# A four-layer convolution block: buffers, and the place of side work in its interleaved stages

## The chip, the cores and the metric

The kernel runs on one core of a Trainium2 chip. The metric is the device time of one launch in microseconds (us). Three runs of the kernel before took 5979.35, 5992.16 and 6012.22 us; their median is 5992.16 us.

## The reference

The input x is 16 images of 64 x 64 tokens with 256 channels, all fp32. Four layers follow one another. Each takes the group norm of x (32 groups of 8 channels, over the whole image) and adds its result to x.

```python
def _gn(v, G=32, eps=1e-5):
    ...
# layer 0: the nearest of 1024 code vectors replaces each token
dis = sum(xf*xf) + sum(e*e) - 2 * xf @ e;  out0 = e.T[argmin(dis)]
# layer 1: attention within each image row of 64 tokens, sigmoid instead of softmax
out1 = sigmoid(f @ g.T) @ h          # f, g: 32 channels, h: 256
# layer 2: a rank-one attention over all 4096 tokens of an image
sm = softmax(x0[:, :, None] * x1[:, None, :], axis=1)
out2 = sigmoid(einsum('bn,bnm->bm', x2, sm)) * x
# layer 3: linear attention with 4 heads of 32 channels, then a layer norm
q = softmax(q over channels) * 32**-0.5;  k = softmax(k over tokens)
out3 = layernorm((k v^T)^T q @ w_out + b_out) * gamma + beta
x = x + out_i(_gn(x))                # for i = 0, 1, 2, 3
```

## The kernel before, in words

**Tiling.** An image (a "batch", b = 0 to 15) has 4096 tokens. It is cut into 8 chunks of 512 tokens (`NCHUNK`, `CW`), and a chunk into 4 token tiles of 128 (`CH`, `P`). Between the layers x lies in DRAM in transposed form, one tile of 128 partitions x 2 channel halves x 512 tokens per chunk (512 KB): x1 after layer 0, x2 after layer 1, x3 after layer 2.

**Stages.** Each stage of a batch is a Python generator. It emits instructions and yields a number of units. `stats0` takes the statistics of the input. `stage1` is the search of layer 0: per token tile four matmuls against the codes (line 382), a sum with the negated norms and a maximum on VectorE (line 389), the index of the maximum (line 394), and a gather of the code vector that is added onto the token tile by an indirect DMA of GpSimd (line 395). Its side work per chunk is `norm` (the normalized tile and its squares, lines 327 and 330, and the row norms), `norm_rows` (a small copy, line 348, which the bias of line 377 reads), `back` (transposes of the finished tokens, line 357, their copy, line 360, the statistics and the store of x1) and the two loads `load` and `tokens` (lines 317 and 321). `layer1` computes per chunk f and g (line 465), h (lines 476 to 485), the scores and their sigmoid (lines 494 to 500) in `attend`, then the attention product and the sum in `mix` (lines 509 and 513). `rows2` projects x2 onto three vectors, each chunk into its own 32 columns of PE (line 567). `stage2` goes over 32 token tiles x 2 halves of the image: ScalarE makes 2048 exponentials per partition with their sum (line 619), VectorE multiplies them by the third projection and sums (line 622); both write the same tile `ex`. `gate2` applies the gate (lines 675 and 676) and stores x3. `stage3` is layer 3: a first pass over the chunks computes k, q and v, the exponentials of k with a running maximum, the softmax of q per head, and the sum of k v products; a second pass (`form`, `variance` and the loop after them) makes the output from the stored q tiles, the small matrix `wctx` and x3.

**The q softmax** (lines 768 to 776) takes a maximum on VectorE (770), a subtraction on GpSimd (771), an exponential on ScalarE (772), a sum and a reciprocal on VectorE (774, 775) and a product on GpSimd (776). In the kernel before all of it is emitted in one piece after the transposes of k (line 762) and `queries(ch - 1)`, which transposes the q tile of the chunk before (line 717) and stores it to DRAM through ScalarE's queue.

**What orders the work.** At the end of the kernel a list of tasks gives each stage of each batch a start and a length, in units of one batch. A heap always resumes the task with the smallest time; a resumed task moves on by length x yielded units / total. So the stages of up to five batches are emitted interleaved. `LEN1`, `LENG` and `LEN3` are lengths of layer 1, the gate and layer 3; `total` of layer 1 is 88 in the kernel before. A compile-time scheduler then puts the instructions of each engine in a fixed order: in the order of emission where an instruction is ready by its own estimate, and a later one first where it is not. `tc.high_priority` puts a few ahead (the ends of the group-norm statistics, `gn_finish`, lines 261 to 277). [...] All loads and most stores are issued from SyncE's queue (SP), which waits at an issue whose buffer is not free yet.

**Buffers.** A tile with a `tag` shares `bufs` slots with the others of this tag; a new tile waits for the last reader of its slot. `t4` (5 slots of 4 KB a partition) holds the negated norms `nn` and the distances `nd` of the search, the squares `sq`, layer 1's `fg` and the projections `rows`. `v2` (5 slots of 2 KB) holds layer 3's `kx`, `ek`, `qT` and `qz`. `ex` has 2 slots of 8 KB, `h` 2 of 4 KB, `xb` 3 of 4 KB (loads of the statistics, the rows and layer 3), `qo` 2. The PSUM tiles of 1024 columns (`wide`: `pd` of the search, `ph` and `po` of layer 1) share 2 slots.

Of the kernel before, what the change touches and what calls it, by code (L numbers as in the profile page):

```python
# [35 lines left out]
LAG3, LENG = 0.06, 0.8  # L36
LAG4 = 0.04
LEN3 = {0: 0.4, 1: 0.33, 2: 0.37}
# [3 lines left out]
def kernel(  # L42
# [55 lines left out]
    neg_mat = s1p.tile([P, P], F32, tag="t4", name="neg_mat", bufs=5)  # L98
# [92 lines left out]
    gam = s3p.tile([P, C], F32, tag="v2", name="gam", bufs=5)  # L191
# [116 lines left out]
    def stage1(b):  # L308
# [14 lines left out]
        def norm(ch):  # L323
            xn[ch] = s1p.tile([P, NK, CW], F32, tag="xn", name=f"xn_{tag}_{ch}")
            sq = s1p.tile([P, NK, CW], F32, tag="t4", name=f"sq_{tag}_{ch}", bufs=5)
# [46 lines left out]
        for ch in range(NCHUNK):  # L372
            for t in range(CH):
                T = ch * CH + t

                nn = s1p.tile([P, CODES], F32, tag="t4", name=f"nn_{tag}_{T}", bufs=5)
# [10 lines left out]
                nd = s1p.tile([P, CODES], F32, tag="t4", name=f"nd_{tag}_{T}", bufs=5)  # L387
# [13 lines left out]
                if t == 1:  # L401
                    if ch + 1 < NCHUNK:
                        norm(ch + 1)
                        yield 2
                if t == 2:
                    if ch + 1 < NCHUNK:
                        norm_rows(ch + 1)
                    if ch > 0:
                        back(ch - 1)
                        yield 2  # L410
                if t == 3:
                    if ch + 1 < NCHUNK:
                        tokens(ch + 1)
# [10 lines left out]
    def layer1(b):  # L424
# [34 lines left out]
        def attend(ch):  # L459
# [9 lines left out]
            fg = s1p.tile([2 * CK, 2, HW], F32, tag="t4", name=f"fg_{tag}_{ch}", bufs=5)  # L469
# [3 lines left out]
            ph = wide(f"ph_{tag}_{ch}").rearrange("p (t c) -> p t c", c=C)  # L473
            for t in range(CH):
                for k in range(NK):
                    nc.tensor.matmul(  # L476
                        ph[:, t, :], lhsT=X[:, k, t * P : (t + 1) * P], rhs=wh_n[:, k, :],
                        start=(t % 2 == 0 and k == 0), stop=False, skip_group_check=True,
                    )
                if t % 2 == 1:  # L480
                    nc.tensor.matmul(
                        ph[:, t - 1 : t + 1, :], lhsT=ones3, rhs=h_row, start=False, stop=True, skip_group_check=True
                    )
            hs[ch] = s1p.tile([P, CH, C], F32, tag="h", name=f"h_{tag}_{ch}")
            nc.scalar.copy(hs[ch], ph)
            yield 5
# [203 lines left out]
    def stage3(b):  # L690
# [33 lines left out]
        for ch in range(NCHUNK):  # L724
# [40 lines left out]
            if ch > 0:  # L765
                queries(ch - 1)
# [173 lines left out]
```

## Time and profile before

| | |
|---|---|
| median of three runs | 5992.16 us |
| time of the profiled execution | 5985.76 us |
| its span | 5984.0 us |
| mean granted clock of TensorE | 0.949 |
| busy PE / DVE / ACT / POOL | 5310.6 / 5132.9 / 4756.8 / 1873.7 us |
| instructions on PE / DVE / ACT / POOL | 25167 / 7270 / 7138 / 1314 |
| last search matmul (line 382) | 5209 us |

PE is TensorE's matmuls, PEld its weight loads, DVE VectorE, ACT ScalarE, POOL GpSimd, SP SyncE. The busy time of an engine leaves out its waits. The page lists an engine's idle time by the instruction that stood at the head of its queue and by what ended the wait. An fp32 matmul appears as two records (4096 for the 2048 of the search), a transpose as one. The costliest groups are these (mean ns of one instruction, and how many):

| group | ns | count |
|---|---|---|
| L622 DVE product and sum of the exponentials | 2318 (and 82 for reading the sum) | 1024 |
| L619 ACT exponentials | 2089 (and 190 for reading the sum) | 1024 |
| L382 PE search matmul, records | 621 each, 2013.5 us together | 4096 |
| L389, L394 DVE maximum and its index | 1212, 1218 | 512 each |
| L377 ACT negated norms | 1145 | 512 |

The profile of the steady part repeats from batch to batch: search matmuls of successive batches begin at 3455, 3808, 4162 and 4514 us.

### The profile page before, as it was taken

How to read it: one execution, taken by the hardware profiler on the slowest of the kernel's cores; microseconds unless marked ns; L12 is line 12 of the kernel's file. 1: busy time of each engine (PE TensorE's matmuls, PEld its weight loads, DVE VectorE, ACT ScalarE, POOL GpSimd, SP SyncE). 2: the span in 40 equal slices, each digit the busy share in tenths (PEclk: the TensorE clock that was granted, in tenths of full speed). 3: DMA queues.
4: the chain of work that ended last, by engine and by line, in shares of the span. 5: the costliest groups of instructions: out<-in, count | busy, mean ns of one | idle time of the engine just before them, and what ended most of it. 6: DMA issues, size and time to landing. Idle time of an engine off the chain costs nothing.

```text
span 5984.0 us, 73947 instructions
## 1 busy us (share of the span) xinstructions
PE 5310.6 (89%) x25167; PEld 3208.0 (54%) x25167; DVE 5132.9 (86%) x7270; ACT 4756.8 (79%) x7138; POOL 1873.7 (31%) x1314
## 2 busy tenths in 40 slices
PE   8978798989989899998989989898999989887777
PEld 3535355545556465554646556464655646464445
DVE  6589698899989899898989989898998989888862
ACT  4578597878888797888979788797988879787763
POOL 3222224233332333323333332433333333312231
PEclk9989899999999999999999999999999999998788
DMA  6453645665656657565665746566475655545543
GB/s 185 143 160 112 209 132 186 187 187 158 207 165 201 194 160 227 149 210 163 197 212 156 224 151 207 172 199 203 153 223 160 204 183 172 188 140 176 170 144 111
DMA packets 521359, 1059.10 MB, mean 177 GB/s; under 512 B 52504, under 2 KB 266392, under 8 KB 512792
## 3 DMA queue, kind: packets, MB, share of 16 engines
q1 hardware_dynamic: 406288, 885.11, 44.6%
q0 software_dynamic: 73728, 67.14, 7.8%
q10 hardware_dynamic: 40968, 102.13, 4.5%
q8 instruction: 200, 3.28, 0.2%
q14 instruction: 175, 1.43, 0.1%
HBM read 751.18 MB, written 303.04 MB: 176 GB/s over the span
## 4 chain that ended last, share of the span: by engine, by line
PE 48%; DVE 21%; ACT 15%; issue 7%; DMA 5%; POOL 4%; ACTq 0%; SPq 0%; POOLq 0%; DVEq 0%
PE pd_s L382 16%; DVE ex_s L622 10%; ACT ex_s L619 6%; PE ph_l L476 4%; PE pqv_s L751 4%; PE po_s L849 3%; DVE i_s L394 2%; PE pk_s L729 2%; PE pr_r L567 2%; DVE nd_s L389 2%; PE po_l L509 2%; POOL xc_s L395 2%; PE pvr_s L829 1%; DVE st_s L254 1%; PE pc_s L780 1%
## 5 line engine op out<-in xcount | busy, mean ns | idle before, releaser
L622 DVE CUSTOM_DVE_ANT_0 ex_s<-ex_s,x2b 128x2048 f32<-128x2048 f32 x1024 | 2369.4, 2318 | 135.9 <-ACT ex_s L619 133.5
L619 ACT ACTIVATE ex_s<-x0b,nmax_s,x_r 128x2048 f32<-128x2048 f32 x1024 | 2138.8, 2089 | 64.7 <-DVE num_s L622 55.0
L382 PE MATMUL pd_s<-e,xn_s 128*128 128x512 f32 x4096 | 2013.5, 621 | 87.6 <-DVE m L389 63.8
L395 POOL DMA_INDIRECT xc_s<-in_emb_rows,i_s x512 | 1084.0, 2117 | 1962.9 <-DVE i_s L394 1460.6
L382 PEld LDWEIGHTS pd_s<-e,xn_s 128*128 128x128 f32 x4096 | 750.6, 196 | 830.4 <-issue 655.0
L389 DVE CUSTOM_DVE_ANT_0 nd_s<-pd_s,nn_s 128x1024 f32<-128x1024 f32 x512 | 620.5, 1212 | 114.8 <-PE pd_s L382 85.4
L394 DVE FIND_INDEX8 i_s<-m,nd_s 128x8 uint32<-128x1024 f32 x512 | 623.5, 1218 | 0.0
L377 ACT ACTIVATE nn_s<-ne,nx_s 128x1024 f32<-128x1024 f32 x512 | 585.1, 1145 | 10.6 <-DVE nx_s L348 3.4
L476 PE MATMUL ph_l<-wh_l,xt_l 128*128 128x256 f32 x2048 | 534.6, 396 | 28.6 <-DVE xt_l L513 20.6
L751 PE MATMUL pqv_s<-wqv_s,xk_s 128*128 128x256 f32 x2048 | 491.9, 381 | 2.9 <-ACT xt_s L360 2.9
L476 PEld LDWEIGHTS ph_l<-wh_l,xt_l 128*128 128x128 f32 x2048 | 381.7, 194 | 155.1 <-issue 61.2
L751 PEld LDWEIGHTS pqv_s<-wqv_s,xk_s 128*128 128x128 f32 x2048 | 388.4, 191 | 130.1 <-issue 63.3
L832 POOL TENSOR_TENSOR lrs_s<-lrs_s,mhalf 128x4 f32<-128x4 f32 x128 | 187.6, 1465 | 651.5 <-ACT lrs_s L831 638.0
L849 PE MATMUL po_s<-wctx_s,qo_s 128*128 128x256 f32 x1024 | 329.4, 412 | 63.5 <-ACT y_s L852 59.8
L852 ACT ACTIVATE y_s<-po_s,lrs_s 128x256 f32<-128x256 f32 x512 | 236.0, 470 | 147.5 <-PE po_s L849 104.3
L327 ACT ACTIVATE xn_s<-xt_s,nb_n,s_n 128x512 f32<-128x512 f32 x256 | 202.4, 806 | 108.2 <-DMA xt_s<-in_xT 98.6
L776 POOL TENSOR_TENSOR qv_s<-qv_s,qd_s 128x512 f32<-128x512 f32 x128 | 167.2, 1307 | 385.3 <-DVE qd_s L775 312.8
L509 PE MATMUL po_l<-attn,h_l 128*128 128x128 f32 x2048 | 280.7, 283 | 7.3 <-DVE m L389 5.2
L509 PEld LDWEIGHTS po_l<-attn,h_l 128*128 128x128 f32 x2048 | 259.9, 195 | 45.8 <-issue 22.1
L849 PEld LDWEIGHTS po_s<-wctx_s,qo_s 128*128 128x128 f32 x1024 | 178.0, 199 | 194.5 <-ACT y_s L852 123.9
L729 PE MATMUL pk_s<-xk_s,wk_s 128*128 128x512 f32 x512 | 256.6, 623 | 0.0
L860 DVE TENSOR_TENSOR y_s<-pxo_s,y_s 128x512 f32<-128x512 f32 x256 | 174.1, 683 | 91.4 <-ACT y_s L852 91.3
(197 smaller groups left out, 7707.6 us busy)
## 6 DMA issues: line engine op xcount, KB each, us to landing
xs_s<-in_xT SPq DMA_DIRECT2D x128, 512.0 KB
xt_s<-in_xT SPq DMA_DIRECT2D x128, 512.0 KB
xc_s<-in_x SPq DMA_DIRECT2D x128, 512.0 KB
x_s<-xt_s ACTq DMA_DIRECT2D x128, 512.0 KB
xt_l<-x_s SPq DMA_DIRECT2D x128, 512.0 KB
x_l<-xt_l SPq DMA_DIRECT2D x128, 512.0 KB
xr_r<-x_l SPq DMA_DIRECT2D x128, 512.0 KB
xg_g<-x_l SPq DMA_DIRECT2D x128, 512.0 KB
```

Of the source, the lines that this page charges most:

```text
L377: nc.scalar.activation(nn, ne2, AF.Identity, bias=nx2[ch][:, t : t + 1])
L382: nc.tensor.matmul(pd[:, cols], lhsT=xn[ch][:, k, t * P : (t + 1) * P], rhs=e2[:, k, cols], start=(k == 0), stop=(k == NK - 1),)
L389: nc.vector.tensor_tensor_reduce(out=nd, in0=pd, in1=nn, scale=1.0, scalar=-3.0e38, op0=ALU.add, op1=ALU.max, accum_out=m8[:, 0:1],)
L394: nc.vector.max_index(i8, m8, nd)
L395: nc.gpsimd.indirect_dma_start(out=xc[ch][:, t, :], out_offset=None, in_=emb_rows, in_offset=bass.IndirectOffsetOnAxis(ap=i8[:, 0:1], axis=0),
L476: nc.tensor.matmul(ph[:, t, :], lhsT=X[:, k, t * P : (t + 1) * P], rhs=wh_n[:, k, :], start=(t % 2 == 0 and k == 0), stop=False, skip_grou ...
L509: nc.tensor.matmul(po[:, k, t * P : (t + 1) * P], lhsT=hs[ch][:, t, k * P : (k + 1) * P], rhs=at[:, t, :], start=True, stop=True,)
L619: nc.scalar.activation(ex, x0b, AF.Exp, bias=nmax[:, T : T + 1], scale=x01[:, T, 1:2], accum_out=den[:, h, T : T + 1])
L622: nc.vector.tensor_tensor_reduce(out=ex, in0=ex, in1=x2b, scale=1.0, scalar=0.0, op0=ALU.mult, op1=ALU.add, accum_out=num[:, h, T : T + 1],)
L729: nc.tensor.matmul(pk, lhsT=wk_n[:, k, :], rhs=xt[:, k, :], start=(k == 0), stop=(k == NK - 1))
L751: nc.tensor.matmul(pqv[:, j, :], lhsT=xt[:, k, t * P : (t + 1) * P], rhs=wqv_n[:, k, :], start=(j == 0 and k == 0), stop=False, skip_group ...
L849: nc.tensor.matmul(po[:, j, :], lhsT=qT[:, t * P : (t + 1) * P], rhs=wctx[:, 1, :], start=True, stop=True)
```

## The change

It has these parts.

1. `ex` gets 3 slots; `h`, `t4` and `v2` lose one each (1, 4 and 4); `fg` leaves `t4` for a slot of its own.
2. The softmax of q is split over three places: maximum and subtraction ahead of the transposes of k, the exponential at the end of the chunk, and sum, reciprocal and product (the new function `normalize`) at the start of the next chunk.
3. `rows2` loads chunks in pairs, and the matmuls of the two chunks of a pair alternate.
4. In the search `back` comes a token tile earlier, `norm` a tile later, and `norm_rows` moves to the end of the chunk, beside the loads.
5. Layer 1's `attend` is split into `scores` and `values`; `values` of the next chunk (h) comes after `mix`, and so does the load of the chunk after it.
6. In layer 3's second pass `form` and `variance` of the next chunk come ahead of the output matmuls of this one.
7. Some lengths of the tasks are shorter, and layer 1's total is 104 instead of 88.

The diff, cut to its core (the other lines change only `bufs=5` to `bufs=4` of tags `t4` and `v2`):

```diff
-LAG3, LENG = 0.06, 0.8
+LAG3, LENG = 0.06, 0.6
-LEN3 = {0: 0.4, 1: 0.33, 2: 0.37}
+LEN3 = {0: 0.4, 1: 0.3, 2: 0.35}
...
                 yield 4
-                if t == 1:
-                    if ch + 1 < NCHUNK:
-                        norm(ch + 1)
-                        yield 2
-                if t == 2:
+                if t == 1 and ch > 0:
+                    back(ch - 1)
+                    yield 2
+                if t == 2 and ch + 1 < NCHUNK:
+                    norm(ch + 1)
+                    yield 2
+                if t == 3:
                     if ch + 1 < NCHUNK:
                         norm_rows(ch + 1)
-                    if ch > 0:
-                        back(ch - 1)
-                        yield 2
-                if t == 3:
-                    if ch + 1 < NCHUNK:
                         tokens(ch + 1)
                     if ch + 2 < NCHUNK:
                         load(ch + 2)
...
-        def attend(ch):
+        def scores(ch):
...
-            fg = s1p.tile([2 * CK, 2, HW], F32, tag="t4", name=f"fg_{tag}_{ch}", bufs=5)
+            fg = s1p.tile([2 * CK, 2, HW], F32, tag="fg", name=f"fg_{tag}_{ch}", bufs=1)
...
-            hs[ch] = s1p.tile([P, CH, C], F32, tag="h", name=f"h_{tag}_{ch}")
-            nc.scalar.copy(hs[ch], ph)
-            yield 5
+            yield 4
...
+        def values(ch):
...
+            hs[ch] = s1p.tile([P, CH, C], F32, tag="h", name=f"h_{tag}_{ch}", bufs=1)
+            nc.scalar.copy(hs[ch], ph)
...
-            if ch + 2 < NCHUNK:
-                load(ch + 2)
...
-        yield from attend(0)
-        yield 2
+        yield from scores(0)
+        values(0)
+        yield 3
         for ch in range(NCHUNK):
             if ch > 0:
                 store(ch - 1)
             if ch + 1 < NCHUNK:
-                yield from attend(ch + 1)
-                yield 2
+                yield from scores(ch + 1)
             mix(ch)
+            yield 3
+            if ch + 1 < NCHUNK:
+                values(ch + 1)
+            if ch + 2 < NCHUNK:
+                load(ch + 2)
             yield 3
...
-            for j in range(4):
-                xt = xb.tile([P, NK, CW], F32, tag="xb", name=f"xr_{tag}_{h}_{j}")
-                nc.sync.dma_start(out=xt, in_=x2_d[b][4 * h + j])
-                part = slice(32 * j, 32 * j + 32)
+            for two in range(2):
+                xs = {}
+                for j in range(2 * two, 2 * two + 2):
+                    xs[j] = xb.tile([P, NK, CW], F32, tag="xb", name=f"xr_{tag}_{h}_{j}")
+                    nc.sync.dma_start(out=xs[j], in_=x2_d[b][4 * h + j])
                 for k in range(NK):
-                    nc.tensor.matmul(
-                        pr[part, :], lhsT=wrow_n[:, k, part], rhs=xt[:, k, :], start=(k == 0), stop=(k == NK - 1)
-                    )
+                    for j in xs:
+                        part = slice(32 * j, 32 * j + 32)
+                        nc.tensor.matmul(
+                            pr[part, :], lhsT=wrow_n[:, k, part], rhs=xs[j][:, k, :], start=(k == 0), stop=(k == NK - 1)
+                        )
...
-                    ex = s2p.tile([P, TOK // 2], F32, tag="ex", name=f"ex_{tag}_{h}_{T}", bufs=2)
+                    ex = s2p.tile([P, TOK // 2], F32, tag="ex", name=f"ex_{tag}_{h}_{T}", bufs=3)
...
+        def normalize(ch):
+            q4 = qvs[ch][:, :, 0, :].rearrange("p t (h d) -> p t h d", d=DH)
+            qd = small.tile([P, CH, HEADS], F32, tag="qd", name=f"qd_{tag}_{ch}")
+            nc.vector.tensor_reduce(qd, q4, AX.X, ALU.add)
+            nc.vector.reciprocal(qd, qd)
+            nc.gpsimd.tensor_tensor(q4, q4, qd.unsqueeze(3).to_broadcast([P, CH, HEADS, DH]), ALU.mult)
...
             nc.sync.dma_start(out=xt, in_=x3[ch])
+            if ch > 0:
+                normalize(ch - 1)
...
             yield 5
-            pkt = bank(f"pkt_{tag}_{ch}")
-            for t in range(CH):
-                nc.tensor.transpose(pkt[:, t * P : (t + 1) * P], kx[:, t * P : (t + 1) * P], ident)
-            ek = s3p.tile([P, CH, P], F32, tag="v2", name=f"ek_{tag}_{ch}", bufs=5)
-            nc.scalar.copy(ek.rearrange("p t d -> p (t d)"), pkt)
-            if ch > 0:
-                queries(ch - 1)
...
             nc.gpsimd.tensor_tensor(q4, q4, qm.unsqueeze(3).to_broadcast([P, CH, HEADS, DH]), ALU.subtract)
-            nc.scalar.activation(qv[:, :, 0, :], qv[:, :, 0, :], AF.Exp)
-            qd = small.tile([P, CH, HEADS], F32, tag="qd", name=f"qd_{tag}_{ch}")
-            nc.vector.tensor_reduce(qd, q4, AX.X, ALU.add)
-            nc.vector.reciprocal(qd, qd)
-            nc.gpsimd.tensor_tensor(q4, q4, qd.unsqueeze(3).to_broadcast([P, CH, HEADS, DH]), ALU.mult)
+            pkt = bank(f"pkt_{tag}_{ch}")
+            for t in range(CH):
+                nc.tensor.transpose(pkt[:, t * P : (t + 1) * P], kx[:, t * P : (t + 1) * P], ident)
+            ek = s3p.tile([P, CH, P], F32, tag="v2", name=f"ek_{tag}_{ch}", bufs=4)
+            nc.scalar.copy(ek.rearrange("p t d -> p (t d)"), pkt)
+            if ch > 0:
+                queries(ch - 1)
...
                 nc.vector.tensor_copy(ctxa, pc[:, :P])
+            nc.scalar.activation(qv[:, :, 0, :], qv[:, :, 0, :], AF.Exp)
             yield 5
+        normalize(NCHUNK - 1)
+        yield 3
         queries(NCHUNK - 1)
...
             for pr in range(2):
+                if ch + 1 < NCHUNK:
+                    (form, variance)[pr](ch + 1)
...
-                if ch + 1 < NCHUNK:
-                    (form, variance)[pr](ch + 1)
                 yield 3
...
-        end = task("layer1", b + 1 + LAG1, LEN1 if left and b else 0.35, layer1(b), 88)
+        end = task("layer1", b + 1 + LAG1, (LEN1 if b else 0.2) if left else 0.3, layer1(b), 104)
```

## The prediction

> **What bounds the kernel now.** I read the page's shares first, then three stretches and one batch of the steady part (the stretches: busy time and count of PE, PEld, DVE, ACT, POOL, then PEclk, DMA share, GB/s), then the waits of PE and DVE (total us, times, longest).
>
> ```profile
> PE 5310.6 (89%) x25167; PEld 3208.0 (54%) x25167; DVE 5132.9 (86%) x7270; ACT 4756.8 (79%) x7138; POOL 1873.7 (31%) x1314
> ```
>
> No engine is full, and three are close together. No edit changes the number of instructions, so this row should come back almost the same: what can be won is idle time.
>
> ```profile
> 0.00:750.00 750.00, 624.46 (x2689) 323.78 (x2690) 560.81 (x844) 477.46 (x667) 202.00 (x140) 0.92 0.55 162
> 750.00:5210.00 4460.00, 4094.81 (x19732) 2478.33 (x19731) 4032.08 (x5672) 3748.09 (x5602) 1476.64 (x1003) 0.97 0.60 185
> 5210.00:5984.00 774.00, 591.37 (x2751) 405.88 (x2749) 540.00 (x756) 531.22 (x871) 195.09 (x171) 0.86 0.44 147
> 3808.00:4162.00 354.00, 325.86 (x1573) 199.22 (x1572) 317.76 (x450) 296.01 (x446) 121.22 (x81) 0.97 0.61 187
> ```
>
> PE is idle 126 us before 750 us, 365 us up to the last search matmul (5209 us), and 183 us in the tail. One batch in the middle takes 354 us, of which PE works 326 and DVE 318. A 28 us rest per batch is all that the steady part has to give; the tail gives more per us, for there PE is busy only 76%.
>
> ```profile
> PE pd_s L382 <- DVE m L389: 63.8, 55, 4.4
> PE po_s L849 <- ACT y_s L852: 59.8, 66, 5.0
> PE pq_s L717 <- POOL qv_s L776: 51.7, 15, 9.1
> PE pg_n L264 <- DVE qd_s L775: 49.5, 11, 5.6
> PE pc_s L780 <- ACT ek_s L764: 42.6, 42, 2.4
> ...
> DVE ex_s L622 <- ACT ex_s L619: 133.5, 118, 3.9
> DVE y_s L860 <- ACT y_s L852: 91.3, 60, 5.6
> ...
> DVE qd_s L774 <- ACT qv_s L772: 70.6, 57, 3.0
> ```
>
> PE's idle time is spread over many short hand-overs. The third is the q softmax. The fourth has a misleading name: on the timeline at 3831 to 3837 us the statistics matmul waits while the last x1 tile goes PE, ACT copy, DVE statistics, each behind an exponential; the reciprocal at L775 only ends next to it. I do not count its 49.5 us as won.
>
> [...] the ACT row of the q exponential (L772) waits 134.7 us for POOL's subtraction, 79 times, with exponentials of layer 2 queued behind. [...] L771 takes 1.05 us alone, 1339 ns in the mean and up to 3.17. [...] here the four-tile order of L465 takes 144.3/2048 = 70 ns a matmul against 261 for L476 of the same width. [...]
>
> **The change part by part** (against the span of 5984.0; the run's time 5985.76 has 1.8 us around it).
>
> *q softmax in three steps.* Sub on POOL moves ahead of the k transposes, exp to the chunk's end, sum, reciprocal and multiply into the next chunk, ahead of the transposes that use them. Same counts: one ACT exp of 631 ns, two DVE, two POOL a chunk, no DMA. The in-chunk round trip (0.69 + 1.05 + 0.63 + 0.69 + 0.25 + 1.05 = 4.4 us on the last chunks) leaves PE's path. PE gets pq's 51.7, of which 30.5 lie in the steady part and 21.3 after 5250. Next late are DVE and ACT work in front of the same transposes: I keep 25 and 12. On ACT and DVE 134.7 and 70.6 us of waits go; this is no gain by itself, but feeds the next item.
>
> *Third buffer for the exponentials.* ACT waits 55.0 us for DVE, DVE 133.5 for ACT. A pair costs ACT 2089 + 190 and DVE 2318 + 82 ns, so one more tile lets ACT be late by about 2.4 us unseen; the longest waits are 3.9. In the steady part PE sees this only through the buffers that DVE and ACT give back: L382, L849, L336, L476, L762 and L780 wait there 40 + 32 + 32 + 19 + 19 + 17 = 159 us. I keep somewhat over a quarter, 45; bounds 0 and 110. In the tail the exponentials of the last two batches run from 5181 to 5785 with DVE the fullest; DVE is idle 234 of 774 us there, 96 of it before 5785. Under a third of that, 28, is taken.
>
> *Search, within a chunk.* back (8 transposes, 2 ACT copies, 2 DVE statistics, a store on ACT's queue) one step earlier; norm (5 ACT, 17 short PE records) one later, its row copy (149 ns of DVE) and the two SP loads after step 3. Gains: SP's waits for back (L321, 420.7 us; L317, 401.1 us) shrink, and ACT's wait for xt (98.6 us, half of it before 300 us) should go: 10 on the path. Costs: transposes come a step (4 to 11 us) nearer to the gather; in the trace its landing leads them by 3 to 5 us in batch 0 and 15 to 34 from batch 4, so only batches 0 to 2 pay: 10 (bounds 0, 22). L377 now directly follows the row copy; if DVE is one exponential late, ACT stands 2.3 us with exponentials and copies behind it, 128 times at worst. ACT has 1227 us idle and the third buffer covers one such wait: 10 (bounds 0, 60).
>
> *Rows in pairs.* The 512 matmuls alternate two column tiles. Already 12 run in 1.93 us (161 ns each, not 491 as for L382), so at most 161 - 123 = 38 ns each, 20 us, and likely 5. Each half now waits with 8 instead of 4 matmuls for its fourth tile, whose slot comes free a pair later. On the timeline search matmuls fill that 3.7 us hole; without them it costs 0.65 us x 32 = 21. Taken: -5.
>
> *Layer 1 split.* h after the mix, one h buffer: the ACT copy of h waits for the mix, which stands ahead of the same matmuls on PE anyway. The SP load of chunk ch+2 goes behind h, still 3 units ahead of its use. L476's wait for the mix's DVE sum (20.6) is counted above. 0 (bounds -10, +10).
>
> *form and variance earlier.* Products and 1/sigma come half a chunk sooner; ACT's 36.1 us for L832 shrink. But the q load (SP) starts only when the chunk before has released its slot: 3.6 to 4.05 us, with the first product behind it on PE, and less work between. Cover is other work, or in the last batch the po matmuls if they are queued first; without it 3.7 us x 7 = 26. Taken: -3.
>
> *Lengths.* Layer 1's 90 of 104 units now take 0.61 of a batch instead of 0.69, for batch 0 0.17 instead of 0.35; the gate 0.57 instead of 0.76, so layer 3 starts 0.2 (batch 0: 0.35) sooner. 0.2 of layer 3's 129 us of PE (its rows' sum / 16), 26 us, moves from the tail into the head, where PE and DVE are both idle at 600 to 750 us (33 and 46): head and tail together -25. Against it PE's work bunches: +15 (13 batches, 1.2 each; bounds 0, 130, see the slower rival).
>
> *One t4, one v2 buffer fewer.* fg no longer takes a t4. v2's next kx may wait for a q store issued a chunk ago: +5.
>
> Sum: -37 - 73 - 10 + 10 + 10 - 5 - 3 - 25 + 15 + 5 = -113. Profiled 5985.76 - 113 = 5873; that run lies 6.4 below the median 5992.16, hence 5879 there. I round up to 5885, as every kept share is a judgement.
>
> **The rivals.** *More than the sum*: the loops between ACT, DVE and PE feed each other, and half of the 365 us goes with half of the tail's 183: 5984 - 200 = about 5790. For it: PE, DVE and ACT rest at the same moments. Against: DVE works 318 of the 354 us, so it becomes the bound.
>
> *Nothing*: each short wait gives way to the one behind it, since DVE has only 8 us more rest than PE per batch: gains of 30 in the tail, costs of 25 as above: 5985.
>
> *Slower, by bunching*: PE already has full 25 us slices (25.00 at 3700 and 3850) beside poor ones (19.4 at 3825). With layer 1 and the gate squeezed into the first 0.6 of a batch, PE is the bound there, and exponentials and search leave it idle in the rest. The poor slices (3808 to 3858) lose 10 us per batch; if that doubles, 13 x 10 = 130, and the steady part's kept 70 us are lost in it, so only 43 of the sum remain: 5984 - 43 + 130, about 6070; with half the doubling 6010. It decides once PE's rest per batch rises by over 43/13 = 3.3 us above 28.
>
> *Not doing what it says* is a small one: each engine's order is not the text's (12 rows matmuls, six of search, then 4), so a moved step may stay put; that ends in "nothing".
>
> **How the numbers follow.** Forecast 0.55 (own range 5830 to 5950), more 0.15, nothing 0.15, slower 0.15. Low 5800 cuts half of "more", high 6000 most of "slower": 2 in 10. Within 0.5% means 5962 to 6022, about what a measurement of this kernel can tell from no change. Faster 0.54 + 0.15 = 0.69, same 0.01 + 0.14 = 0.15, slower 0.16 with a part of "nothing".
>
> **What would show it.** Right: busy sums within 1%; PE's pq wait under 20 us; DVE's ex wait under 80; ACT's L772 wait under 30; a middle batch of 345 to 349 us; search ending near 5130. Wrong: transposes waiting over 60 us for gathers, L377 waiting for L348 over 100, pz waiting for q loads over 60, or a middle batch of 354 or more. A middle batch unchanged with a tail of 700 us would leave only the tail's part.

## The result, and the profile after

The changed kernel is slower: 6145.83 us in the median of six runs (6138.82 to 6170.64) against 5988.65 us for six runs of the kernel before beside it, a ratio of 1.0267 (95% interval 1.0241 to 1.0293). The forecast was 5885 us, with 0.16 for slower. The profiled execution has a span of 6142.6 us, 158.6 more than before, at a mean PE clock of 0.939 of full speed instead of 0.949.

First the page's busy row of the changed kernel.

```profile
PE 5372.4 (87%) x25167; PEld 3230.4 (53%) x25167; DVE 5151.9 (84%) x7270; ACT 4754.2 (77%) x7138; POOL 1960.2 (32%) x1314
```

The counts are those of before. PE nevertheless works 62 us longer on the same matmuls. Then the stretches (busy time and count of PE, PEld, DVE, ACT, POOL, then PEclk, DMA share, GB/s), cut where they were cut before, with the end as a fourth.

```profile
0.00:750.00 750.00, 622.69 (x2646) 319.34 (x2647) 556.76 (x842) 472.44 (x668) 199.43 (x141) 0.91 0.55 162
750.00:5210.00 4460.00, 4059.43 (x19531) 2454.95 (x19531) 3977.13 (x5563) 3689.59 (x5522) 1553.60 (x988) 0.97 0.59 182
5210.00:5984.00 774.00, 566.25 (x2458) 368.54 (x2457) 578.73 (x794) 543.98 (x844) 179.74 (x147) 0.82 0.43 145
5984.00:6143.00 159.00, 123.98 (x536) 87.56 (x534) 39.32 (x73) 48.19 (x106) 27.47 (x38) 0.85 0.28 96
```

Up to 5210 us PE has issued 244 matmul records fewer than before (43 in the first stretch, 201 in the second), at almost the same clock: it fell behind a little in both. In the third stretch its clock is 0.82 where it was 0.86. I split every span of this study in the same way, by the first and last distance operations of the batches: the head (from the first distance operation of all to the first of batch 7), the mean batch from there to batch 15, and the tail (last search operation to the end). Before: 2035, 352.5, 773 us. After: 2088, 357.6, 825. So the loss lies in all three: 53 us, 8 x 5.1, 52, and the rest, 13 us, in the last search batch.

The waits of PE, then of DVE, then of ACT, in the changed kernel (total us, times, longest):

```profile
PE pz_s L833 <- DMA qo_s<-qd_s: 138.5, 72, 5.7
PE pg_n L264 <- DVE mv_n L261: 90.8, 15, 23.6
PE pd_s L382 <- DVE m L389: 77.0, 44, 5.4
...
PE pr_r L572 <- DMA xr_r<-x_l: 49.0, 24, 4.7
...
PE pq_s L729 <- POOL qv_s L723: 14.7, 5, 7.7
```

```profile
DVE y_s L874 <- ACT y_s L866: 211.9, 120, 5.2
DVE x_r L582 <- PE prt_r L581: 105.0, 31, 13.8
...
DVE ex_s L627 <- ACT ex_s L624: 69.6, 78, 1.8
```

```profile
ACT rows_r L576 <- PE pr_r L572: 151.4, 32, 14.8
ACT qv_s L796 <- POOL qv_s L778: 150.8, 80, 6.6
```

Two waits that the change aimed at did fall: PE for the q softmax (51.7 to 14.7) and DVE for exponentials (133.5 to 69.6). That the parts aimed at them lowered them is not said by this; a4, b2 and d3 below speak against it. A new wait leads the list: pz, the product in `form`, waits 138.5 us for its q tile. This is its line in the kernel before:

```profile
PE pz_s L821 <- DMA qo_s<-qd_s: 11.6, 15, 3.0
```

DVE's wait at y_s, the output of layer 3, went from 91.3 to 211.9. The rows of layer 2 have doubled or tripled their waits, on PE (18.7 before), ACT (69.1) and DVE (35.5).

The chain of work that ended last shows the first of these in the last batch (start, us, what):

```profile
6065.29 0.62 PE po_s L863 x2
6065.92 0.02 issue
6065.94 3.71 DMA qo_s<-qd_s
6069.65 0.14 issue
6069.78 2.04 PE pz_s L833 x2
6071.82 0.85 PE po_s L863 x2
...
6075.98 0.62 PE po_s L863 x2
6076.60 0.02 issue
6076.62 3.31 DMA qo_s<-qd_s
6079.93 0.14 issue
6080.06 2.05 PE pz_s L833 x2
```

Read it from the top: the last output matmul (po) of chunk ch-1 sets the q slot free, 0.02 us later the load of chunk ch+1 starts, and PE stands still until it lands, for form now comes ahead of the output matmuls of chunk ch. Of two q buffers one belongs to chunk ch, so there is nothing between release and use.

### The profile page after: what moved, and what is told of

It reads as the page before. It is cut to its first block, busy times and chain, and to the rows that moved or that the text cites. A ratio compares the mean times of both kernels' runs of the same rounds, so it can differ in the third digit from the quotient of the medians.

```text
span 6142.6 us, 73811 instructions
## 1 busy us (share of the span) xinstructions
PE 5372.4 (87%) x25167; PEld 3230.4 (53%) x25167; DVE 5151.9 (84%) x7270; ACT 4754.2 (77%) x7138; POOL 1960.2 (32%) x1314
## 5 line engine op out<-in xcount | busy, mean ns | idle before, releaser
L627 DVE CUSTOM_DVE_ANT_0 ex_s<-ex_s,x2b 128x2048 f32<-128x2048 f32 x1024 | 2382.7, 2333 | 69.8 <-ACT ex_s L624 69.6
L382 PE MATMUL pd_s<-e,xn_s 128*128 128x512 f32 x4096 | 2018.7, 625 | 83.0 <-DVE m L389 77.0
L382 PEld LDWEIGHTS pd_s<-e,xn_s 128*128 128x128 f32 x4096 | 755.4, 197 | 861.9 <-issue 715.4
L377 ACT ACTIVATE nn_s<-ne,nx_s 128x1024 f32<-128x1024 f32 x512 | 583.2, 1142 | 24.9 <-DVE nx_s L348 15.5
L490 PEld LDWEIGHTS ph_l<-wh_l,xt_l 128*128 128x128 f32 x2048 | 396.1, 199 | 162.5 <-DVE xt_l L512 67.6
L863 PE MATMUL po_s<-wctx_s,qo_s 128*128 128x256 f32 x1024 | 353.3, 435 | 11.7 <-ACT y_s L866 11.2
L874 DVE TENSOR_TENSOR y_s<-pxo_s,y_s 128x512 f32<-128x512 f32 x256 | 175.2, 686 | 211.9 <-ACT y_s L866 211.9
L723 POOL TENSOR_TENSOR qv_s<-qv_s,qd_s 128x512 f32<-128x512 f32 x128 | 193.5, 1512 | 431.2 <-DVE qd_s L722 276.7
L833 PE MATMUL pz_s<-qo_s,gram_s 128*128 128x512 f32 x256 | 166.0, 735 | 145.6 <-DMA qo_s<-qd_s 138.5
L743 PE MATMUL pk_s<-xk_s,wk_s 128*128 128x512 f32 x512 | 273.2, 655 | 0.0
L863 PEld LDWEIGHTS po_s<-wctx_s,qo_s 128*128 128x128 f32 x1024 | 190.9, 209 | 146.4 <-issue 79.3
```

The lines of the kernel that those rows point to most:

```text
L377: nc.scalar.activation(nn, ne2, AF.Identity, bias=nx2[ch][:, t : t + 1])
L382: nc.tensor.matmul(pd[:, cols], lhsT=xn[ch][:, k, t * P : (t + 1) * P], rhs=e2[:, k, cols], start=(k == 0), stop=(k == NK - 1),)
L490: nc.tensor.matmul(ph[:, t, :], lhsT=xt[ch][:, k, t * P : (t + 1) * P], rhs=wh_n[:, k, :], start=(t % 2 == 0 and k == 0), stop=False, skip ...
L627: nc.vector.tensor_tensor_reduce(out=ex, in0=ex, in1=x2b, scale=1.0, scalar=0.0, op0=ALU.mult, op1=ALU.add, accum_out=num[:, h, T : T + 1],)
L743: nc.tensor.matmul(pk, lhsT=wk_n[:, k, :], rhs=xt[:, k, :], start=(k == 0), stop=(k == NK - 1))
L863: nc.tensor.matmul(po[:, j, :], lhsT=qT[:, t * P : (t + 1) * P], rhs=wctx[:, 1, :], start=True, stop=True)
```

## The experiments

The theory after reading this: the early form stalls on the q load, and the new lengths put layer 3 beside work it collides with; softmax and third buffer do little. The main rival: no part is at fault by itself, and any new order of these interleaved stages loses about a per cent against one that was tuned. Ratios are to the kernel before, run on the same chip; head, batch and tail are of each profiled execution, in us. The profiled executions of a3, c2 and c3 took 28, 16 and 14 us more than the median of their runs, that of b1 18 less, so their stages are compared with that margin.

| kernel | ratio (95% interval) | head | batch | tail |
|---|---|---|---|---|
| before | 1 | 2035 | 352.5 | 773 |
| the change | 1.0267 (1.0241 to 1.0293) | 2088 | 357.6 | 825 |
| a1: change, form back | 1.0166 (1.0146 to 1.0187) | 2098 | 358.6 | 758 |
| a2: before, form ahead alone | 1.0164 (1.0143 to 1.0186) | 2055 | 360.2 | 805 |
| a3: change, old lengths | 1.0071 (1.0054 to 1.0088) | 2033 | 357.8 | 811 |
| a4: before, softmax in three steps alone | 1.0083 (1.0066 to 1.0101) | 2044 | 358.5 | 768 |
| b1: change, form back, old lengths | 0.9927 (0.9911 to 0.9944) | 2022 | 349.5 | 743 |
| b2: b1, q softmax in one piece | 0.9942 (0.9925 to 0.9958) | 2036 | 353.1 | 738 |
| b3: before, LAG4 0.05 | 1.0003 (0.9991 to 1.0016) | 2041 | 353.3 | 759 |
| b4: before, LAG1 0.07 | 1.0165 (1.0148 to 1.0182) | 2063 | 363.7 | 771 |
| c1: a3, three q buffers, two for exponentials | 0.9866 (0.9848 to 0.9883) | 2053 | 348.8 | 708 |
| c2: b1, layer 1's new lengths | 0.9847 (0.9826 to 0.9868) | 2027 | 349.4 | 742 |
| c3: b1, new gate and layer 3 lengths | 1.0119 (1.0085 to 1.0153) | 2063 | 362.7 | 744 |
| c4: b1, two buffers for exponentials | 0.9917 (0.9899 to 0.9935) | 2054 | 347.5 | 741 |
| d1: c3, layer 3 back in its place | 0.9914 (0.9888 to 0.9941) | 2016 | 351.6 | 732 |
| d2: the parts that pay | 0.9878 (0.9849 to 0.9908) | 2050 | 349.1 | 717 |
| d3: c4, search moves undone | 1.0116 (1.0089 to 1.0142) | 2051 | 359.7 | 764 |
| d4: c4, layer 1 in one piece | 1.0044 (1.0033 to 1.0056) | 2051 | 355.8 | 750 |

### Form and variance ahead: a1, a2, c1

a1 is the changed kernel with

```diff
             for pr in range(2):
-                if ch + 1 < NCHUNK:
-                    (form, variance)[pr](ch + 1)
...
+                if ch + 1 < NCHUNK:
+                    (form, variance)[pr](ch + 1)
                 yield 3
```

> The kernel after with one part undone: form and variance of layer 3's second pass stand again behind the output matmuls. Theory 'q load exposed' (PE waits 138.5 us for the q loads at pz in the kernel after, 17.7 before[...]): the pz wait falls under 30 us, PE's busy sum falls by 30 us or more, and the time by 90 to 150 us, to about 6000 to 6055. Rival 'bunching' (the shorter lengths cost it): the pz wait goes and others grow in its place; time falls by under 40 us, 6105 or more.

a2 is the reverse: the kernel before with these lines moved ahead, and nothing else.

```diff
             for pr in range(2):
+                if ch + 1 < NCHUNK:
+                    (form, variance)[pr](ch + 1)
...
-                if ch + 1 < NCHUNK:
-                    (form, variance)[pr](ch + 1)
                 yield 3
```

> The kernel before with that one part alone: form and variance ahead. Theory 'q load exposed': pz waits 100 us or more for the q loads, and the time rises by 80 to 150 us, to 6070 to 6140. Rival 'bunching': with the old lengths the q loads have more other work beside them, pz waits under 60 us and the time stays within 30 us of 5989.

Measured: 1.0166 and 1.0164. (The 17.7 us of the first expectation count the weight loads' waits too; PE's matmuls waited 11.6.) The part costs some 1.0% in the changed kernel and 1.6% alone. PE's waits in a2, then in a1:

```profile
PE pz_s L821 <- DMA qo_s<-qd_s: 123.3, 53, 5.3
```

```profile
PE pz_s L833 <- DMA qo_s<-qd_s: 24.4, 23, 2.7
```

The wait comes and goes with the part. In a2 it is 112 us longer than before, and the span is 111 us longer (6094.8 against 5984.0), but these two do not answer each other one to one: all of PE's idle time grew by 79 us only, and its busy time by 32, as its mean clock fell from 0.949 to 0.942. It hurts most in the tail, where PE has little else to do: of the 138.5 us in the changed kernel, 78 belong to the second passes of the last four batches, and the chain has such loads in three bunches (from 5663, 5881 and 6066 us). The first seven chunks of the last batch (pz to pz) take 46.5 us together before, 71.8 with the change, 47.4 in a1.

c1 takes the cause away and leaves form ahead. A third q tile takes the room of the third exponential, so that one goes back to two (c4 below shows what that alone does):

```diff
-            qs[ch] = s3p.tile([P, CW], F32, tag="qo", name=f"qo_{tag}_{ch}")
+            qs[ch] = s3p.tile([P, CW], F32, tag="qo", name=f"qo_{tag}_{ch}", bufs=3)
```

> The kernel after with the old lengths, form and variance still ahead, but three buffers for the loaded q tiles (tag qo), so that a load need not wait for the chunk before; to make room the exponentials have two buffers. Theory 'q load exposed by its buffer': pz waits under 40 us for the q loads (143 with two buffers), the tail goes from 811 us back under 770, and the time comes within 0.5% of c4, which has form behind and also two buffers of exponentials. Rival 'the place of form itself, not the load': pz's wait may go, but the time stays 1% or more above c4.

Measured: 0.9866, from a3's 1.0071. PE's group of form products in c1 (count, busy, mean ns, idle before and what ended it), and the chain of its last batch:

```profile
L833 PE MATMUL pz_s<-qo_s,gram_s 128*128 128x512 f32 x256 | 166.2, 736 | 7.1 <-ACT gram_s L825 3.9 <-ACT y_s L866 1.4 <-DMA qo_s<-qd_s 1.2
```

```profile
5884.82 0.86 PE pz_s L833 x2
5885.68 0.43 PE po_s L863 x2
...
5886.77 0.66 PE po_s L863 x2
5887.43 0.79 PE pvr_s L841 x8
5888.21 0.54 PE po_s L863 x2
...
5889.40 0.61 PE po_s L863 x2
5890.02 0.86 PE pz_s L833 x2
```

The load has left the chain, 1.2 us of waiting for it remain in the whole kernel, and the chunk shown takes 5.2 us of PE work without a hole; the seven chunks take 38.0. So form ahead is sound, and the missing buffer made it a loss. Against c4, which differs from c1 only in form's place and the q buffer, the two together gain 0.5%: 0.9866 against 0.9917. A third q buffer with form behind was not tried.

### The lengths: a3, b1, c2, c3, d1

a3 is the changed kernel with the old lengths (91 units stand for the 88 of before, as the split layer has more of them):

```diff
-LAG3, LENG = 0.06, 0.6
+LAG3, LENG = 0.06, 0.8
-LEN3 = {0: 0.4, 1: 0.3, 2: 0.35}
+LEN3 = {0: 0.4, 1: 0.33, 2: 0.37}
...
-        end = task("layer1", b + 1 + LAG1, (LEN1 if b else 0.2) if left else 0.3, layer1(b), 104)
+        end = task("layer1", b + 1 + LAG1, LEN1 if left and b else 0.35, layer1(b), 91)
```

> The kernel after with its lengths undone (gate 0.8, layer 3 as before, layer 1 spread over the same share of a batch as before: total 91 for its 90 units). Theory 'q load exposed': the time falls by under 40 us, to 6105 or more, and pz still waits over 100 us. Rival 'bunching': the steady period goes from 358 us back to 352 or less, and the time falls by 90 us or more, to 6055 or less.

b1 is a1 and a3 together: both diffs.

> The kernel after with form/variance back behind the output matmuls and the old lengths. If the two costs add (1.0% and 2.0% by the runs before), the ratio to the kernel before is 0.996 to 1.000, near 5985. Rival 'any new schedule costs' (the kernel before sits at a tuned point: its steady period is 350.6 us, every variant so far 357 to 359, whatever was changed): the period stays at 356 to 359 us and the ratio at 1.005 to 1.012.

Measured: 1.0071 and 0.9927. Without these two parts the change is a gain of 0.7%, and the lengths cost 1.95% with form ahead (1.0267 to 1.0071) and 2.4% without (1.0166 to 0.9927). c2 and c3 put one half of them each into b1. c2:

```diff
-        end = task("layer1", b + 1 + LAG1, LEN1 if left and b else 0.35, layer1(b), 91)
+        end = task("layer1", b + 1 + LAG1, (LEN1 if b else 0.2) if left else 0.3, layer1(b), 104)
```

> b1 (form behind, old lengths; 0.9927) with layer 1's lengths of the kernel after alone: 0.2 for batch 0, 0.3 for the last, total 104. All lengths together cost 2.4% there (b1 to a1). If layer 1's bunching is the cost: ratio 1.01 or more. If the gate's and layer 3's are: ratio under 1.000.

c3:

```diff
-LAG3, LENG = 0.06, 0.8
+LAG3, LENG = 0.06, 0.6
-LEN3 = {0: 0.4, 1: 0.33, 2: 0.37}
+LEN3 = {0: 0.4, 1: 0.3, 2: 0.35}
```

> b1 with the gate's length 0.6 and layer 3's last lengths of the kernel after alone. If the shorter gate is the cost (layer 3 begins 0.2 of a batch sooner, where layer 1 and the search already fill PE): ratio 1.01 or more. If layer 1's lengths are: under 1.000.

Measured: c2 0.9847, a gain of 0.8% on b1; c3 1.0119, slower than b1 by 1.9%. The halves do not add: together they would cost 1.1%, and they cost 2.4%. What is left over is open, and so is the gain of c2, whose profile shows no stage in which it wins. In c3 PE's idle time per batch is 36.4 us, against 23.7 in b1. The gate's work is the same; but layer 3 is started by its planned end, so it starts 0.2 of a batch sooner. d1 leaves the gate short and gives layer 3 its old start:

```diff
-        task("layer3", end + LAG4, LEN3.get(left, 1.0), stage3(b), 160)
+        task("layer3", end + LAG4 + (0.2 if left > 1 else 0), LEN3.get(left, 1.0), stage3(b), 160)
```

> c3 (b1 with the gate's length 0.6 and the shorter LEN3) with layer 3 delayed by 0.2 of a batch again, except in the last two batches, so that it begins where it did with the gate's length 0.8. Theory 'layer 3's place' (its first pass at 0.66 to 1.06 of a batch and its second at 0.18 to 0.48, beside layer 1, instead of 0.87 to 1.27 and 0.39 to 0.68): the period returns from 362.7 to under 352 us and the ratio to within 0.4% of b1's 0.9927. Rival 'squeezed gate': it stays at 1.006 or more.

Measured: 0.9914. The loss of c3 is gone, so it was layer 3's place. The matmuls of layer 2's rows run from about 0.76 to 0.84 of a batch (counted from the first distance operation of its search) in all these kernels. Those of layer 3's first pass begin at 0.85 before and 0.86 in d1, behind the rows; in the changed kernel at 0.65 and in c3 at 0.63, and so over the rows, in c3 over the end of layer 1 (0.68) too. PE's waits in c3, then in d1:

```profile
PE pd_s L382 <- DVE m L389: 68.1, 56, 8.2
PE pr_r L572 <- DMA xr_r<-x_l: 54.2, 31, 7.4
PE ph_l L490 <- DVE xt_l L512: 53.9, 22, 4.2
```

```profile
PE pd_s L382 <- DVE m L389: 39.4, 28, 8.2
...
PE pr_r L572 <- DMA xr_r<-x_l: 24.5, 15, 3.7
```

The third of these lines is down to 5.7 us in d1. ACT waits for rows 151.4 us in c3 and 92.9 in d1. That layer 3 shares SP's queue, DVE and ACT with rows and layer 1 there fits these lines; which of the three shared resources decides was not separated.

### Softmax and the third buffer: a4, b2, c4

a4 is the kernel before with only the q softmax of the change (normalize as a function of its own, the exp at the chunk's end).

```diff
+        def normalize(ch):
...
+            if ch > 0:
+                normalize(ch - 1)
...
-            nc.scalar.activation(qv[:, :, 0, :], qv[:, :, 0, :], AF.Exp)
...
+            nc.scalar.activation(qv[:, :, 0, :], qv[:, :, 0, :], AF.Exp)
             yield 5
```

> The kernel before with the q softmax in three steps alone (same buffers, same lengths). By the forecast: PE's wait at pq for POOL falls from 51.7 to under 20 us, time falls by 20 to 50 us, to 5940 to 5970. Rival 'the waits only move': PE's wait at pq falls, other waits take its place, within 15 us of 5989. Rival 'the exponential at the chunk's end is later on ACT': up to 30 us slower.

b2 undoes just that in b1.

```diff
-            if ch > 0:
-                normalize(ch - 1)
...
+            nc.scalar.activation(qv[:, :, 0, :], qv[:, :, 0, :], AF.Exp)
+            qd = small.tile([P, CH, HEADS], F32, tag="qd", name=f"qd_{tag}_{ch}")
+            nc.vector.tensor_reduce(qd, q4, AX.X, ALU.add)
...
-            nc.scalar.activation(qv[:, :, 0, :], qv[:, :, 0, :], AF.Exp)
             yield 5
```

> As the run before it, with the q softmax in one piece again; what is left of the change is the third buffer of the exponentials, the rows in pairs, the moves in the search, layer 1's split and the lost buffers. If parts add: 0.8% less than the run before it, ratio 0.987 to 0.993. Rival 'any new schedule costs': ratio 1.00 to 1.012, period 355 us or more.

Measured: a4 1.0083; b2 0.9942 beside b1's 0.9927, whose intervals overlap. Worth between nothing and a small gain in one setting, and a loss in the other. PE's wait for the q softmax in a4, then ACT's:

```profile
PE pq_s L724 <- POOL qv_s L718: 57.5, 23, 9.0
```

```profile
ACT qv_s L791 <- POOL qv_s L773: 136.1, 82, 6.1
```

Neither fell (51.7 and 134.7 before). In b1, with the split, PE's wait is even longer than in b2 without it:

```profile
PE pq_s L729 <- POOL qv_s L723: 44.8, 15, 12.6
```

```profile
PE pq_s L722 <- POOL qv_s L781: 25.7, 5, 11.6
```

It is 43.7 us in a3, and 14.7, 13.9 and 18.8 in the changed kernel, a1 and c3: it is short where layer 3 starts early. So the fall in the changed kernel goes with the lengths, not with the split. In chunks 30 to 99 the exp starts 0.0 us (median) after POOL's subtraction, as before: moved down in the text, it still stands on ACT in front of later work and waits there, the 136.1 us above. And the slack between the product and the transposes became smaller, 14.0 us in the median before, 6.2 in a4, since sum, reciprocal and multiply now come only in the next chunk.

c4 is b1 with `bufs=2` for the exponentials:

```diff
-                    ex = s2p.tile([P, TOK // 2], F32, tag="ex", name=f"ex_{tag}_{h}_{T}", bufs=3)
+                    ex = s2p.tile([P, TOK // 2], F32, tag="ex", name=f"ex_{tag}_{h}_{T}", bufs=2)
```

> b1 with two buffers for the exponentials instead of three. By the forecast's step the third buffer is worth 73 us (1.2%): ratio 1.003 to 1.007. If it does little because ACT and DVE wait for other things: within 0.3% of b1's 0.9927.

Measured: 0.9917 beside 0.9927. The third buffer is worth nothing that can be measured here. DVE's wait for exponentials is 83.1 us with two buffers and 58.6 with three: shorter, and the time is no better for it.

### Search and layer 1: d3, d4

d3 undoes the moves of the search in c4 (norm back to t == 1, norm_rows and back to t == 2):

```diff
-                if t == 1 and ch > 0:
-                    back(ch - 1)
-                    yield 2
-                if t == 2 and ch + 1 < NCHUNK:
-                    norm(ch + 1)
-                    yield 2
-                if t == 3:
+                if t == 1:
+                    if ch + 1 < NCHUNK:
+                        norm(ch + 1)
+                        yield 2
+                if t == 2:
                     if ch + 1 < NCHUNK:
                         norm_rows(ch + 1)
+                    if ch > 0:
+                        back(ch - 1)
+                        yield 2
```

> c4 (0.9917) with the search's moves undone. By the forecast (gain 10, costs 20 us) undoing them should win 0.0 to 0.3%: 0.988 to 0.992. Rival 'the moves make c4's gain' (earlier back frees the buffers that SP waits for): 0.996 or more.

d4 puts layer 1 back into one piece in c4 (attend for scores and values, two h buffers, load behind the mix, a total of 88):

```diff
-        def scores(ch):
+        def attend(ch):
...
-            yield 4
...
+            hs[ch] = s1p.tile([P, CH, C], F32, tag="h", name=f"h_{tag}_{ch}")
+            nc.scalar.copy(hs[ch], ph)
+            yield 5
```

> c4 (0.9917) with layer 1 in one piece again (attend, two buffers of h, the load behind mix, total 88 for its 87 units). By the forecast the split is worth nothing (bounds 10 us either way): within 0.3% of 0.9917. Rival 'the split makes c4's gain' (two PSUM tiles of 1024 columns are shared by the search and layer 1, and h and mix now take them one after the other): 0.997 or more.

Measured: d3 1.0116 and d4 1.0044 against c4's 0.9917. In this setting the search moves gain 2.0% and the split 1.3%, the two best parts of the change. ACT's wait for the search's x in c4, then in d3:

```profile
ACT xn_s L327 <- DMA xt_s<-in_xT: 21.3, 13, 4.1
```

```profile
ACT xn_s L327 <- DMA xt_s<-in_xT: 113.7, 48, 5.8
```

DVE's wait for exponentials goes the same way, 83.1 us with the moves and 139.1 without, both with two buffers: its fall in the changed kernel is not the third buffer's alone. SP's wait for the transposes of back (L321) is 287.0 us with them and 548.1 without; but at the same line its wait for the gathers is 251.4 with and 71.4 without, so the two together differ by 81 us only. The gathers cost PE 78.2 us in c4 and 37.2 in d3; PE waits less in c4 at the statistics (29.6 against 80.5, L264 for L261), at the transposes of q (31.8 against 65.6, for the softmax) and at those of k (13.0 against 50.4, for ACT's exponentials). Which of these carries the gain is not shown, and the moves were not tried one by one. For the split, PE in c4 and in d4:

```profile
PE pd_s L382 <- DVE m L389: 23.7, 17, 3.4
```

```profile
PE pd_s L382 <- DVE m L389: 89.2, 46, 2.7
```

The distance matmuls of the search wait for a free wide PSUM tile; layer 1's h takes one from the same ring, and in one piece it asks for it together with the scores. That this wait is the price of d4 is an argument and not shown, for the same wait is longest in c2, one of the two fastest kernels:

```profile
PE pd_s L382 <- DVE m L389: 122.5, 48, 5.6
```

### How much a schedule's place alone does: b3, b4

Both shift stages of the kernel before by a hundredth of a batch, 3.5 us, with no other edit.

```diff
-LAG4 = 0.04
+LAG4 = 0.05
```

> The kernel before with LAG4 at 0.05 instead of 0.04: layer 3 is emitted one hundredth of a batch later, nothing else. Rival 'any new schedule costs': the period goes to 355 us or more and the time rises by 0.5 to 1.5%. If the parts' own mechanisms make the difference: within 0.3% of the kernel before.

```diff
-LAG1, LEN1 = 0.06, 0.7
+LAG1, LEN1 = 0.07, 0.7
```

> The kernel before with LAG1 at 0.07 instead of 0.06: layer 1 and all that follows it of a batch are emitted one hundredth of a batch later against the search. Same two expectations as for the run before it: 0.5 to 1.5% slower and a period of 355 us or more under 'any new schedule costs', within 0.3% otherwise.

Measured: b3 1.0003, b4 1.0165. The first moves layer 3 alone and is free; the second moves layer 1 and all that follows it against the search. PE's waits in b4:

```profile
PE pg_n L264 <- DVE mv_n L261: 76.8, 14, 11.8
PE px_s L336 <- ACT sq_s L330: 68.6, 36, 10.0
PE po_s L849 <- ACT y_s L852: 65.7, 60, 5.0
```

Before, they are 34.9, 41.4 and 59.8. A batch takes 363.7 us instead of 352.5: PE is idle for 32.9 instead of 28.0, and works 330.8 instead of 324.5; the mean clock of the whole execution is 0.935 instead of 0.949. Why this shift and not the other is open. The rival falls as a rule, for b3 costs nothing and b1, c1, c2, c4 and d1 beat the kernel before; but a single part measured at one place, as a4, d3 and d4 are, carries an uncertainty of the size of b4. The cost of form and that of the lengths were each seen in more than one setting, and each was undone (c1, d1).

### The parts that pay: d2

c1 with layer 1's new lengths:

```diff
-        end = task("layer1", b + 1 + LAG1, LEN1 if left and b else 0.35, layer1(b), 91)
+        end = task("layer1", b + 1 + LAG1, (LEN1 if b else 0.2) if left else 0.3, layer1(b), 104)
```

> The kernel after with the old gate and layer 3 lengths, three q buffers and two of the exponentials: form ahead as in c1 (0.9866), layer 1's lengths as in c2 (0.8% better than b1). If the two add: ratio 0.978 to 0.982. Rival 'places of stages interact': 0.985 or more.

Measured: 0.9878, between nothing and a small loss on c1: layer 1's new lengths, a gain on b1, are none here, and the gains of c1 and c2 do not add. Those two stay the fastest kernels of the study, 5918.78 and 5911.20 us beside 6000.91 for the kernel before; their intervals overlap.

## Why the prediction was wrong, point by point

It was wrong in sign. Two of its steps failed, two gains were put too high, and two parts that it put at nothing gained.

**Form and variance earlier: the step that failed first.** It named the mechanism, a load that "starts only when the chunk before has released its slot", and the price without cover, 3.7 us x 7 = 26. Then it took -3, on the argument that other work or queued output matmuls cover it. In the last batch nothing does. Its seven chunks there take 71.8 - 46.5 = 25 us more, which looks like the uncovered price of 26, but the match is luck: the wait for q loads grew by 17 us (18.4 against 1.7), PE's work by 11 (49.9 us against 38.8, at a mean clock of 0.74 against 0.93, which the prediction had no term for), and a wait of 5 us for ACT's y_s went away. The second passes of the last four batches wait 17 to 23 us each, and those of batches 1 to 10 still 5.0 on average. The output matmuls cannot be the cover, because form was moved ahead of just these. Predicted -3, measured +60 (1.0% of 6000) in the changed kernel, and +100 alone. The prediction's own sign of being wrong, pz waiting over 60 us for q loads, came true.

**Lengths: the step that failed second.** It counted layer 3's earlier start as a gain of 25, out of head and tail, against 15 for bunching. Measured: about +140 for all the lengths (0.9927 in b1, 1.0166 in a1), and +115 for the gate's and layer 3's alone (1.0119 in c3). The head became longer with the new lengths, 2022 to 2098 us from b1 to a1, and the tail too, 743 to 758. What failed is the overlap: the sum let layer 3 run earlier, over the rows and the end of layer 1, for 15 us of bunching; with its old start the cost is gone (d1). The slower rival looked at the right part with a range of 0 to 130; its place, layer 1 and gate in the first 0.6 of a batch, was not the one. A shorter gate with layer 3 where it was costs nothing (d1), and layer 1's lengths alone even gain (c2). Its point of decision, 3.3 us more PE rest per batch, is passed in c3 (36.4 against 28.0); in the changed kernel the rest is 30.1 and the point is not reached, though it lost more, for PE also works 3.0 us longer in a batch, and the tail has its q loads. The middle batch (357.6, wrong sign from 354) and the end of the search (last matmul at 5316 us, 5130 forecast) did tell.

**Third buffer: -73 was mis-sized**, measured about nothing (b1 beside c4). The sum took a quarter of the waits that PE has for buffers from DVE and ACT. The wait of DVE did fall below 80, as the sign asked, but more by the search moves (139.1 in d3, 83.1 in c4) than by the buffer (58.6 in b1), and the buffer's share of it bought no time.

**Softmax: -37 was mis-sized**, measured -13 with overlapping intervals (b2 to b1) to +47 (a4). PE's wait is 14.7 in the changed kernel, as the sign asked, but alone it does not fall at all, and with the old lengths the split does not shorten it. ACT's wait, forecast under 30, is 150.8. The prediction itself had noted that each engine's order is not the text's, and then moved the exp on paper all the same.

**Search: 10 - 10 = 0 and layer 1: 0** were too small. ACT's xt wait did go, as the search step said (98.6 to 22.0), and neither gathers (48.2) nor L377 behind the row copy (15.5 us for L348) reached the wrong signs. Gathers passing 60 us would not have told: they cost PE 75.5 us in c1 and 78.2 in c4, which are faster than the kernel before. Layer 1's step did not name the wide PSUM tiles. With 119 and 76 us, by d3 and d4, these two parts are the largest gains seen here, though of the size that a place alone may add (b4: 100 us). Together they are 195 us, and c4 as a whole gains 52: so the parts do not add here either, or others cost.

**Rows in pairs and the lost buffers** were not tried alone. PE's wait for the rows' loads rises with layer 3's place (54.2 us in c3) and falls back with it (24.5 in d1, 18.7 before); that leaves little for the pairs themselves. What the lost buffers cost is open.

**The sum.** Without form and lengths the steps came to -100; b1 measured -46 (5949.87 against 5995.63). The sign was right there, but by luck: the softmax and the third buffer, for which the forecast had 110 us, gave next to nothing (b2, c4), and the gains that were seen came from the parts put at 0. The busy sums, promised within 1%, missed for PE by 1.2%, about what its clock lost (0.939 of 0.949), and for POOL by 4.6%, half of it in the softmax subtractions, 1668 ns in the mean instead of 1339.

## What to carry to other kernels

When a consumer is moved ahead of the work that used to stand between a buffer's release and its next use, count the buffers first: with two, the load itself became the link here (3.3 to 3.7 us in five of the last batch's chunks), and the cure was one more tile of that kind (1.2 us of waiting left in c1), not of the kind whose wait is largest in the list. A wait that is long in the list of an engine with rest to spare need not be a price (here DVE's for exponentials: 83.1 us in c4 and 58.6 in b1, at ratios of 0.9917 and 0.9927), and one in the list of the fullest engine need not be one either, as c2 shows (122.5 us at L382, ratio 0.9847); undo the part and measure. In a pipeline of stages laid over one another, a shorter stage moves its successors, so say what the successor now lies beside before counting an earlier start as a gain. Split a bundle of edits into parts, as here two bad ones hid a gain.

## What was not expected of the hardware

In the last batch of the changed kernel PE lost more than its waits. Stretches there (columns as above, PEclk the third from the end): the first is a wait for a q load, the next two are the work that follows it.

```profile
6066.00:6069.70 3.70, 0.00 (x0) 0.00 (x0) 0.69 (x1) 0.42 (x1) 0.00 (x0) 0.94 0.96 318
6069.70:6073.00 3.30, 3.22 (x8) 1.93 (x9) 0.69 (x1) 0.23 (x1) 0.00 (x0) 0.55 0.12 40
6073.00:6076.60 3.60, 3.59 (x22) 2.43 (x19) 0.69 (x1) 1.46 (x4) 1.01 (x1) 1.00 0.00 0
```

The clock is 0.55 for 3.3 us after a wait of 3.7, and the two records of pz take 2.04 us where they take 0.86 in c1's chain. Over the seven chunks PE works 49.9 us instead of 38.8 before, at a mean clock of 0.74 instead of 0.93: some 1.6 us more per chunk, on top of the load. Why the clock is lower there is not shown. In the whole kernel the same 25167 matmul records are 62 us busier at a mean clock of 0.939 instead of 0.949; if busy time goes as one over the clock, 5310.6 us x 0.949 / 0.939 is an estimated 57 us longer. The load itself took 3.3 to 3.7 us in five of the last batch's six loads on this chain, and 2.56 in the last.
